# When to count the next chunk's neighbours: one visit in a chunk's last step

## The chip, the cores and the metric

The kernel runs on one core of a Trainium2 chip. The metric is the device time of one execution in microseconds (us). Three executions of the kernel before took 240.62, 241.02 and 240.00 us; the median is 240.62 us.

## The reference

Two layers of a graph network with residual and layer norm, on 4096 nodes with 64 features and a dense 0/1 adjacency matrix of 4096 x 4096, some 0.4% of it ones. Cut to what matters:

```python
# layer 0: each row's last 100 neighbours, weighted by 0.5 ** (rank from the end)
rank = jnp.cumsum(mask, axis=1)
deg = rank[:, -1:]
k = jnp.minimum(deg, 100.0)
pos = rank - (deg - k)
w = mask * jnp.where(pos > 0, 0.5 ** (k - pos), 0.0)
x = layernorm(x + (w @ (x @ weight) + bias))
# layer 1: mean over neighbours and self, linear map, relu, L2 norm
deg = sum(adj, axis=1) + 1
h = (adj @ x + x) / deg
z = relu(concat([x, h], 1) @ W + b)
x = layernorm(x + z / max(norm(z), 1e-12))
```

The weight of an edge depends on how many neighbours of its row have a higher column number. So a block of the matrix can be weighed only when the blocks of higher columns have been counted.

## The kernel before

**Tiles and steps.** The matrix is handled transposed, in 64 tiles of 512 rows (a slab g, 0 to 7) by 512 columns (k, 0 to 7). Within a slab k runs from 7 down to 0, slabs run from 0 to 7, and each tile is one step: `when[g, k]` gives the step number i, 0 to 63. A tile is read from HBM as float32 and stored as bf16 (512 KB) by a DMA that GpSimd (POOL) issues (`load_next`, L97 to L104). Eight loads are issued ahead, then one at the start of every step, so step i issues load i + 8. There are 32 tile buffers; later loads wait until the tile that holds the buffer has been used for the last time, which is in a sum of layer 1.

**Chunks.** The tiles of a slab are grouped into chunks (`chunks`, L84): one tile each in slabs 0 and 1, chunks of 1, 1, 2, 2, 2 in slab 2, chunks of two in slabs 3 and 4, and of four in slabs 5 to 7. All tiles of a chunk share one `near`: how many neighbours the row has beyond this chunk, capped. The chunk's own tiles lie close enough together that the ordering inside it is worked out from the tile itself.

**What a chunk needs before its first weighing.** `count` (L243) multiplies each of its tiles by `pick` (four matmuls a tile, 128 rows by 32 columns, into the PSUM tile `cnt`). After the chunk's last count DVE adds the result to the running sums (`cs`, L257, or L259 for the first chunk of a slab). `spread` (L262) multiplies `cs` by `further` (PSUM tile `rep`, L265), and ACT turns that into `near` (L267). `cnt`, `rep` and three small products of the epilogue (`pz`, `px`, `pu`) share two PSUM buffers in rotation.

**A step.** The order on each engine is written out by hand. On TensorE (PE) a step is: the counts of its share of the next chunk; `weigh` (L269), 16 matmuls with `tri` (L277) and 16 with `mine` and `near` (L286), 32 x 32 array tiles each, into PSUM `v`; four matmuls of layer 1 where any are ready (`some_sums`, L338, `acc_part`, L313); the `spread` if the share ended the chunk; `gather` (L299, `acc`, L304), the product of layer 0 with the step before's weights; and epilogue pieces of the slab before (`pz`, `px`, `pu`). ACT and DVE each turn half of `v` into weights `w` (L293, L294). PSUM holds `v` of one step, so a step's weighing waits until both halves of the step before's `w` are out. Where no sum of layer 1 was ready and a spread is due, half of the gather is placed ahead of the spread.

**Epilogue of layer 0.** It is spread over the eight steps that follow a slab: `pz` and `y` in the second step of the next slab, `mv` in the third, a square root `s` (ACT) and `r` (DVE) in the fourth, `x1` in the fifth, `hi` and `xl` in the sixth, `lo` and `px` in the seventh, `x1T` and `pu` in the eighth, `c1` one later. After step 63 the remaining sums of layer 1 and its epilogue follow, in an order written out by hand.

The line in the step loop that deals out the counts is L541; `ahead` is the next chunk:

```python
shares = {1: [ahead], 2: [ahead[:2], ahead[2:]], 4: [[], ahead[:2], [], ahead[2:]]}[len(chunk)]
```

In a chunk of two, the first step counts the first two tiles of the next chunk and the second step what is left of it; in a chunk of four, the second step counts two tiles and the fourth the other two.

Of the kernel before, what the change touches and what calls it, by code (L numbers as in the profile page):

```python
# [39 lines left out]
def adj_resnorm_kernel(  # L40
# [42 lines left out]

    chunks = []  # L84
    for g in range(NG):
        sizes = [1] * 8 if g < 2 else [1, 1, 2, 2, 2] if g == 2 else [2] * 4 if g < 5 else [4] * 2
        k = NK
        for n in sizes:
            chunks.append([(g, k - 1 - i) for i in range(n)])
            k -= n  # L90
# [6 lines left out]
    def load_next(n=1):  # L97
        for _ in range(n):
            s = next(loads, None)
            if s is None:  # L100
                return
            g, k = s
            a = a16p.tile([P, KB, R], BF16, tag="a16", name=f"a16_{g}_{k}")
            nc.gpsimd.dma_start(out=a, in_=adjT[g, k])  # L104
            A[g][k] = a
# [137 lines left out]
    def count(g, k, first, last):  # L243
        if first:
            cnt[g] = ps_m.tile([P, R], F32, tag="m", name=f"cnt_{g}_{k}")
        for q in range(KB):
            nc.tensor.matmul(  # L247
                cnt[g][quarters[q], :],
                lhsT=pick[:, PW - 4 * k : PW - 4 * k + Q],
                rhs=A[g][k][:, q, :],  # L250
                start=first,
                stop=last,
            )
        if last:
            new = one.tile([P, R], BF16, tag="cs", name=f"cs_{g}_{k}")
            if g in cs:
                nc.vector.tensor_tensor(new, cnt[g], cs[g], ALU.add)  # L257
            else:
                nc.vector.tensor_copy(new, cnt[g])  # L259
            cs[g] = new  # L260

    def spread(g, k):  # L262

        pr = ps_m.tile([P, R], F32, tag="m", name=f"rep_{g}_{k}")
        nc.tensor.matmul(pr, lhsT=further, rhs=cs[g], start=True, stop=True)  # L265
        near[g] = epi.tile([P, R], BF16, tag="near", name=f"near_{g}_{k}")
        nc.scalar.activation(near[g], pr, AF.Relu, bias=most, scale=-1.0)  # L267

    def weigh(g, k, nr):  # L269

        w = wp.tile([P, KB, R], I16, tag="w", name=f"w_{g}_{k}")
        v = [ps_v.tile([P, 2, R], F32, tag="v", name=f"v_{g}_{k}_{i}") for i in range(2)]
        for q in range(KB):
            for e in range(4):
                nc.tensor.matmul(  # L277
                    v[e // 2][quarters[q], e % 2, :],
                    lhsT=tri[quarters[e], :],
                    rhs=A[g][k][quarters[e], q, :],  # L280
                    start=True,
                    stop=False,
                )
        for q in range(KB):
            for e in range(4):
                nc.tensor.matmul(  # L286
                    v[e // 2][quarters[q], e % 2, :],
                    lhsT=mine[quarters[e], 4 * k + q, :],
                    rhs=nr[quarters[e], :],
                    start=False,  # L290
                    stop=True,
                )
        nc.scalar.activation(w[:, 0:2, :], v[0], AF.Relu, bias=less)  # L293
        nc.vector.tensor_scalar(w[:, 2:4, :], v[1], -STEP * MAX_NEIGH, 0.0, ALU.add, ALU.max)  # L294
        return w
# [3 lines left out]
    def gather(g, k, w, q0=0, q1=KB):  # L299
        if (k, q0) == (NK - 1, 0):  # L300
            acc0[g] = ps_a.tile([P, R], F32, tag="acc0", name=f"acc0_{g}")
        for q in range(q0, q1):
            b = k * KB + q
            nc.tensor.matmul(  # L304
                acc0[g],
                lhsT=xhl[:, b, :],
                rhs=w[:, q, :].bitcast(BF16),
                start=(k, q) == (NK - 1, 0),
                stop=(k, q) == (0, KB - 1),
            )  # L310
# [19 lines left out]
    def evict_part(g):  # L330
        acc = acc1.pop(g)
        if g in part:
            nc.vector.tensor_tensor(part[g], acc, part[g], ALU.add)
        else:
            part[g] = const.tile([P, R], F32, name=f"part_{g}")
            nc.scalar.copy(part[g], acc)

    def some_sums(i, n):  # L338

        done = None  # L340
        while n and todo and done is None and ready(i, todo[0][0], todo[0][1]):
            g, b, first, last = todo.pop(0)
            if first:
                acc1[g] = ps_a.tile([P, R], F32, tag="acc1", name=f"acc_part_{g}_{b}")
            second(acc1[g], g, b, first, last)
            n -= 1
            if last:
                done = g
        return done
# [55 lines left out]
    def first_hT(g):  # L405
        ep["hT", g] = epi.tile([P, R], F32, tag="hT", name=f"hT0_{g}")
        nc.scalar.copy(ep["hT", g], acc0[g])
# [76 lines left out]
    def run(i, engine):  # L484
        for fn, args in hooks.pop((i, engine), []):
            fn(*args)
# [36 lines left out]
    def warm(n):  # L523

        a = A[0][NK - 1][:, 0, :]
        for i in range(n):
            nc.tensor.matmul(pi, lhsT=a[:, 0:P], rhs=a, start=True, stop=True)  # L527
# [10 lines left out]
    for c, chunk in enumerate(chunks):  # L538
        ahead = chunks[c + 1] if c + 1 < len(chunks) else []

        shares = {1: [ahead], 2: [ahead[:2], ahead[2:]], 4: [[], ahead[:2], [], ahead[2:]]}[len(chunk)]  # L541
        nr = near[chunk[0][0]]
        for (g, k), share in zip(chunk, shares):
            i = when[g, k]
            run(i, ACT)
            load_next()
            run(i, POOL)

            w = weigh(g, k, nr) if i == 0 else None
            for s in share:  # L550
                count(*s, s == ahead[0], s == ahead[-1])
            w = w or weigh(g, k, nr)
            run(i, "ACT, late")
            if i == 0:
                warm(4)
            n_todo = len(todo)
            done = some_sums(i, QUOTA)
            half = 0
            if share and share[-1] == ahead[-1]:
                if held is not None and len(todo) == n_todo:  # L560

                    half = KB // 2
                    gather(*held, 0, half)
                spread(*ahead[-1])
            if i == 0:
                warm(3)
            if done is not None:
                evict_part(done)
            if held is not None:
                gather(*held, half)  # L570
            held = (g, k, w)
            if g > 0 and k == NK - 1:
                first_hT(g - 1)
            run(i, PE)
            run(i, DVE)
# [389 lines left out]
```

## Time and profile before

| what | value |
|---|---|
| median of three executions | 240.62 us |
| profiled execution, its own time | 242.02 us |
| its span, first to last instruction | 239.9 us |
| PE busy (matmuls) | 216.0 us, 90% |
| DVE busy | 177.5 us, 74% |
| ACT busy | 134.2 us, 56% |
| POOL busy | 83.4 us, 35% |
| mean granted TensorE clock | 0.967 |
| tile loads: number, median from issue to landing | 64, 15.8 us |

The busy time is an average over stages with different limits, so the stages have to be read one by one: the row of slices cuts the span into 40 equal parts and gives the busy share of each engine in tenths. The list of waits names for each waiting instruction what ended its wait. The timeline shows instructions in order of time: start, duration, engine, line, operation, output and inputs, count, and in brackets the idle time before it with what ended it.

### The profile page before, as it was taken

Reading aid. Unit: us, or ns where it says so; the run is one execution under the profiler, and the core shown is the slowest. Engines: PE = TensorE matmul, PEld = TensorE weight load, DVE = VectorE, ACT = ScalarE, POOL = GpSimd, SP = SyncE. Lnnn points to the kernel's source line nnn. Section 1 sums busy time; section 2 is a strip of 40 time slices with the busy share of each in tenths; the row PEclk is TensorE's granted clock in tenths of the full one; section 3 lists DMA queues with packets and bytes.
Section 4 is the critical chain, followed back from the end, with each engine's and each line's share of the span. In section 5 each row is a group of like instructions: output and inputs, shape, how many; then the busy total and the mean of one; then the engine's idle time right before and its main releaser. Section 6 shows DMA issues by size and latency. Waiting matters only on the chain.

```text
span 239.9 us, 7440 instructions
## 1 busy us (share of the span) xinstructions
PE 216.0 (90%) x3167; PEld 95.9 (40%) x3167; DVE 177.5 (74%) x453; ACT 134.2 (56%) x201; POOL 83.4 (35%) x160
## 2 busy tenths in 40 slices
PE   8689989999789999999999999899999999999810
PEld 2223324244323442443344334443443355676700
DVE  5458888977578689579857975686568866679983
ACT  5058876787357637665555455545555641163493
POOL 8334584331430140221223132313371000168960
PEclk9799999999899999999999999999999999999975
DMA  6999999999999999999899999999990000000021
GB/s 202 211 210 222 210 213 214 221 215 214 221 213 214 216 219 214 214 213 187 163 171 179 165 189 197 178 156 195 209 190 9 0 3 0 3 0 25 0 87 66
DMA packets 11984, 37.33 MB, mean 156 GB/s; under 512 B 1328, under 2 KB 3504, under 8 KB 11952
## 3 DMA queue, kind: packets, MB, share of 16 engines
q0 software_dynamic: 9216, 33.56, 72.6%
q1 hardware_dynamic: 2736, 3.31, 4.2%
q8 instruction: 24, 0.39, 0.6%
q14 instruction: 8, 0.07, 0.1%
HBM read 69.37 MB, written 1.05 MB: 293 GB/s over the span
## 4 chain that ended last, share of the span: by engine, by line
PE 53%; DMA 22%; DVE 11%; POOL 6%; ACT 4%; issue 2%; ACTq 0%; POOLq 0%; DVEq 0%
DMA a<-in_adjT_dram 22%; PE acc L304 14%; PE acc_part L313 13%; PE v L277 7%; PE cnt L247 4%; PE v L286 4%; ACT w L293 3%; PE va L313 2%; DVE w L294 2%; POOL r L377 2%; PE pi L527 2%; PE pz L413 2%; PE rep L265 2%; POOL rn L377 2%; PE va L658 1%
## 5 line engine op out<-in xcount | busy, mean ns | idle before, releaser
L293 ACT ACTIVATE w<-v,less 128x1024 int16<-128x1024 f32 x64 | 71.3, 1115 | 56.3 <-PE v L286 42.5
L294 DVE TENSOR_SCALAR w<-v 128x1024 int16<-128x1024 f32 x64 | 78.3, 1223 | 24.9 <-PE v L286 23.8
L104 POOL DMA_DIRECT2D a<-in_adjT_dram x64 | 36.0, 564 | 103.6 <-PE acc_part L313 44.4
L304 PE MATMUL acc<-w,xhl 128*128 128x512 bf16 x256 | 70.1, 384 | 0.0
L313 PE MATMUL acc_part<-a,x1hl 128*128 128x512 bf16 x156 | 40.5, 382 | 0.0
L304 PEld LDWEIGHTS <-xhl 128*128 128x128 f16 x256 | 23.1, 98 | 35.4 <-issue 12.0
L313 PEld LDWEIGHTS <-x1hl 128*128 128x128 f16 x224 | 18.6, 98 | 30.6 <-issue 13.8
L277 PE MATMUL v<-a,tri 32*32 32x512 bf16 x1024 | 29.5, 388 | 0.7 <-ACT w L293 0.6
L267 ACT ACTIVATE near<-rep,most 128x512 bf16<-128x512 f32 x35 | 23.9, 683 | 9.1 <-PE rep L265 9.1
L247 PE MATMUL cnt<-a,pick 128*32 128x512 bf16 x256 | 22.1, 387 | 7.0 <-DMA a<-in_adjT_dram 6.5
L286 PE MATMUL v<-near,mine 32*32 32x512 bf16 x1024 | 28.3, 380 | 0.0
L257 DVE TENSOR_TENSOR cs<-cnt,cs 128x512 bf16<-128x512 f32 x27 | 18.5, 685 | 8.8 <-PE cnt L247 8.8
L277 PEld LDWEIGHTS <-tri 32*32 32x32 bf16 x1024 | 9.8, 88 | 22.2 <-issue 21.6
L265 PE MATMUL rep<-cs,further 128*128 128x512 bf16 x35 | 13.8, 393 | 2.2 <-DVE cs L257 2.1
L377 POOL TENSOR_TENSOR rn<-ss,power 128x4 f32<-128x4 f32 (+1 forms) x5 | 6.3, 1277 | 26.2 <-DVE ss L680 26.2
L247 PEld LDWEIGHTS <-pick 128*32 128x32 bf16 x256 | 5.1, 93 | 21.7 <-issue 15.2
L232 POOL TENSOR_TENSOR a<-a,ident_b 128x128 bf16<-128x128 bf16 x32 | 12.7, 428 | 0.1
L286 PEld LDWEIGHTS <-mine 32*32 32x32 bf16 x1024 | 9.9, 88 | 1.8 <-issue 1.8
L658 PE MATMUL va<-wts,hT 128*128 128x64 f32 x64 | 8.0, 276 | 2.2 <-ACT hT L631 1.1
L259 DVE CAST cs<-cnt 128x512 bf16<-128x512 f32 x8 | 5.5, 690 | 5.4 <-PE cnt L247 5.4
L209 POOL TENSOR_TENSOR xr<-c,xhl 128x256 f32<-128x256 f32 x8 | 5.3, 664 | 11.7 <-ACT xhl L207 11.6
L747 ACT ACTIVATE u<-u,off,r 128x64 f32<-128x64 f32 x24 | 8.6, 431 | 0.8 <-POOL off L736 0.8
(136 smaller groups left out, 236.9 us busy)
## 6 DMA issues: line engine op xcount, KB each, us to landing
a<-in_adjT_dram POOLq DMA_DIRECT2D x64, 512.0 KB, 15.8
c<-in_x_quads_dram SPq DMA_DIRECT2D x2, 512.0 KB, 4.5
x<-in_x_dram SPq DMA_DIRECT2D x8, 128.0 KB, 6.4
out_dram<-u SPq DMA_DIRECT2D x8, 128.0 KB, 1.7
wts<-in_weights_dram SPq DMA_DIRECT2D x1, 160.0 KB, 7.2
```

The source lines that it names most:

```text
L104: nc.gpsimd.dma_start(out=a, in_=adjT[g, k])
L247: nc.tensor.matmul(cnt[g][quarters[q], :], lhsT=pick[:, PW - 4 * k : PW - 4 * k + Q], rhs=A[g][k][:, q, :], start=first, stop=last,)
L257: nc.vector.tensor_tensor(new, cnt[g], cs[g], ALU.add)
L265: nc.tensor.matmul(pr, lhsT=further, rhs=cs[g], start=True, stop=True)
L267: nc.scalar.activation(near[g], pr, AF.Relu, bias=most, scale=-1.0)
L277: nc.tensor.matmul(v[e // 2][quarters[q], e % 2, :], lhsT=tri[quarters[e], :], rhs=A[g][k][quarters[e], q, :], start=True, stop=False,)
L286: nc.tensor.matmul(v[e // 2][quarters[q], e % 2, :], lhsT=mine[quarters[e], 4 * k + q, :], rhs=nr[quarters[e], :], start=False, stop=True,)
L293: nc.scalar.activation(w[:, 0:2, :], v[0], AF.Relu, bias=less)
L294: nc.vector.tensor_scalar(w[:, 2:4, :], v[1], -STEP * MAX_NEIGH, 0.0, ALU.add, ALU.max)
L304: nc.tensor.matmul(acc0[g], lhsT=xhl[:, b, :], rhs=w[:, q, :].bitcast(BF16), start=(k, q) == (NK - 1, 0), stop=(k, q) == (0, KB - 1),)
L313: nc.tensor.matmul(acc, lhsT=x1hl[:, b, :], rhs=A[g][b // KB][:, b % KB, :], start=first, stop=last)
L377: nc.gpsimd.tensor_tensor(r, v, power[:, 0:n], ALU.pow)
```

## The change

Two edits. The counts of the next chunk are all made in the last step of a chunk, in one visit, ahead of that step's weighing, and the spread follows in the same step. For a chunk of one nothing changes; for a chunk of two the counts move from its first step to its second; for a chunk of four the first half joins the second half in the fourth step. And slab 4's last two chunks of two become one chunk of four.

```diff
-        sizes = [1] * 8 if g < 2 else [1, 1, 2, 2, 2] if g == 2 else [2] * 4 if g < 5 else [4] * 2
+        sizes = {0: [1] * 8, 1: [1] * 8, 2: [1, 1, 2, 2, 2], 3: [2] * 4, 4: [2, 2, 4]}.get(g, [4, 4])
...
-        shares = {1: [ahead], 2: [ahead[:2], ahead[2:]], 4: [[], ahead[:2], [], ahead[2:]]}[len(chunk)]
+        shares = [[]] * (len(chunk) - 1) + [ahead]
```

## The prediction

> **What bounds the kernel now.** I read the slices first. The profile row for DMA tells where transfers run without a gap, PEclk where TensorE went cold.
>
> ```profile
> PE   8689989999789999999999999899999999999810
> PEclk9799999999899999999999999999999999999975
> DMA  6999999999999999999899999999990000000021
> GB/s 202 211 210 222 210 213 214 221 215 214 221 213 214 216 219 214 214 213 187 163 171 179 165 189 197 178 156 195 209 190 9 0 3 0 3 0 25 0 87 66
> ```
>
> A slice is 6.0 us. Until 108 us (18 slices) the queue moves 202 to 222 GB/s without a break; then the rate falls to 156 to 209 while PE stays full. So there are two stages: up to about 74 us a tile's landing sets the pace (the chain of waits has DMA pieces from 24.4 to 63.1 us), afterwards PE does, up to 210 us. The list of waits then says what each engine waited for (total us, times, longest):
>
> ```profile
> PE cnt L247 <- DMA a<-in_adjT_dram: 6.5, 9, 2.2
> PE rep L265 <- DVE cs L257: 2.1, 3, 1.1
> POOL a L104 <- PE acc_part L313: 44.4, 20, 4.6
> ```
>
> PE's only large wait is that of a count for a tile not yet landed. POOL's 44.4 us says that late loads are issued when a sum of layer 1 frees a buffer, so they follow PE. The timeline shows the wait that this change moves:
>
> ```profile
> 60.92 0.40 PE L247 MATMUL cnt<-a,pick 128*32 128x512 bf16 x4
> 63.06 0.40 PE L247 MATMUL cnt<-a,pick 128*32 128x512 bf16 x4 [1.74 <-DMA a<-in_adjT_dram]
> 63.39 0.46 PE L277 MATMUL v<-a,tri 32*32 32x512 bf16 x16
> ...
> 71.17 0.38 PE L265 MATMUL rep<-cs,further 128*128 128x512 bf16 x1 [1.10 <-DVE cs L257]
> ...
> 152.55 0.40 PE L247 MATMUL cnt<-a,pick 128*32 128x512 bf16 x4 [0.62 <-DMA a<-in_adjT_dram]
> ```
>
> At 60.92 PE is in step 18 (steps are numbered from 0, eight to a slab; pz of slab 1 at 59.91 marks step 17). It counts tiles 20 and 21, waits 1.74 us for tile 21, and its own weighing, whose tile is long there, stands behind the count. At 152.55 (step 49) the first half of a split visit waits for tile 53.
>
> **The Trainium skill.** "TensorEngine Tiling (Array Packing)", Key Properties: changing the tiling mode drains TensorE. The trace agrees: a visit with one tile moves the next operation by 0.33 us (20.38 to 20.71), one with two tiles by 0.54 (101.73 to 102.27). So a tile costs 0.21 and a visit 0.12 beside it. "TensorE: Matmul & The Clock Gate", Part 1: an idle stretch throttles the clock. After the 1.74 us the granted clock in 60 to 66 us is 0.81. The same page, Architectural detail: ScalarE and VectorE take instructions strictly in order. In the trace near always follows its step's w (104.15 after 103.07 plus 1.11).
>
> **Part 1, what goes away.** Visits before: 18 chunks of one tile, 11 of two, six of four in two visits: 41. After: 18 + 9 + 7 = 34. Seven visits at 0.12 are 0.84 us of PE. One chunk fewer saves a spread (0.22 us of PE: acc starts 0.22 after rep), a cs on DVE (0.69) and a near on ACT (0.68). All 256 count matmuls stay. SP's and POOL's instructions and their order stay; only when buffers come free moves.
>
> **Part 2, the landing wait, steps 18 to 24.** Chunks of two were counted in their predecessor's first step and now in its last, one step later. Load n+8 waits until load n has landed, so POOL's issue times give landings: tile 21 at 63.06 (the count), 22 at 66.0, 23 at 68.5, 24 at 71.3, 25 at 73.7. These stay. I walk PE with the durations of the timeline: tri and mine 0.58 from start to next operation, four gathers or sums 0.86, ACT's w ends 1.91 after v starts, DVE's 2.09.
> - Step 18: v at 60.95 instead of 63.39, gather to 62.4.
> - Step 19 counts tiles 20 and 21: waits from 62.6 to 63.06; v 63.4. DVE first ends mv (63.9), then cs (64.6), so rep 64.7, near 65.6 to 66.3 (behind w and the square root).
> - Step 20: v waits for w of step 19 (65.9), mine for near (66.35).
> - Step 21 counts 22, 23: waits for 68.5, v 68.8, rep 69.9, near to 71.45.
> - Step 22: mine waits for near (71.5), gather and px to 73.1. Step 23 counts 24, 25: waits for 73.7, v 74.1, sums, rep, gather, pu to 77.0.
> - Step 24: v at 77.1 against 79.95 before. But before, tiles 26 and 27 had been counted then (0.54), and the spread is level. Net gain 2.3.
>
> **Part 3, steps 25 to 36.** Steps 27 to 29 have no sums to run, and there ACT and DVE set the pace: w alone takes 1.91 to 2.09 of a step whose PE work is 1.53. Now cs and near of the next chunk fall into steps 27 and 29 with the square root, r and hi: rep at 27 and at 29 waits some 0.4 each for cs, mine at 28 and 30 some 0.2 for near, and v at 28 and 30 for DVE's w. Step 31's v comes at 97.65 against 99.08; one spread of 0.22 is behind, so the gain is down to 1.2. Step 35 now counts four tiles, in 0.97 us from 109.4; the last, tile 39, lands at 109.0 (load 39 issued at 101.0, 8.0 to landing), just in time. Step 37's v: 115.1 against 116.4, gain **1.3** (the spread saved is in it).
>
> **Part 4, steps 37 to 63.** PE-bound, sums in every step, and the visits at 39, 43, 47 and so on already ended with spread in the last step, so near's chain is as before. Six visits go (39, 41, 45, 49, 53, 57): 6 x 0.12 = 0.7. The visit at 49 took 1.35 us from 151.53 to 152.88 instead of 0.54; that 0.8 goes, if no later count waits in its place. Step 51 needs tile 55: issued at 151.04, landed 6.8 later, 157.8; counted at 158.69. The step 49 work that goes shortens the lead from 7.65 to about 7.0 at the last tile's turn, against 6.8: it just holds. Tile 51 at step 47 (issued 139.41, 6.5 to landing) has about 6.2 and waits 0.3. Sum: 0.7 + 0.8 - 0.3 = **1.2**, rounded down to 1.1.
>
> **What is not shown.** The waits of near at a chunk's first step are bounded by 0 (hidden) and by 0.68 each (whole near exposed); I take 0.2 to 0.45 from the walk in the four boundaries without sums and 0 elsewhere, because with sums near ends 2.57 us after v (104.84) and mine of the next step starts 2.86 after. The landing waits of slabs 5 to 7 lie between 0 and 1.0 per visit (the 0.62 seen, and more if the queue backs up); I take 0.3 in all. They can also be under today's: 0.2 at 145.5 may vanish. POOL's adds may lengthen a DVE operation by up to 0.8 (q_l took 0.97 at 68.88 against 0.16 at 91.21); the same either way.
>
> **Sum.** 1.3 + 1.1 = 2.4 us. The profiled execution took 242.02 us (span 239.9 and 2.1 around it), 1.4 above the median of 240.62; its 2.4 us are taken off the median: **238.2**. What follows 182 us (own sums, last epilogue) moves earlier as a whole: it has no load left to wait for.
>
> **Rivals.**
> 1. The chain costs are hidden too (ACT and DVE catch up as mv and x1 no longer share steps with cs). The waits of part 2 and 3 that I charged come to about 2.0 (0.8 for cs, 1.2 for near). Without them: 236.2. For it: y and mv stood beside cs in one step (86 to 90 us). Against: 1.10 at 71.17 shows that this chain is already exposed. Chance 0.12.
> 2. The landing wait only moves. Steps 19, 21, 23 wait at the same landings, and what PE did earlier is lost by ACT and DVE before 100 us. Then only part 4 is left, 0.5 to 1.2: 239.4 to 240.1. For it: transfers run unbroken to 108 us, so no landing moves. Against: from 74 us a PE step takes 2.4 to 2.9 us and a tile 2.45, so PE keeps its lead. Chance 0.19.
> 3. Slower: spread in the last step puts count, cs, rep and near in a row before the next weighing, behind ACT's w, at each of the nine boundaries that a chunk of two now leaves this way. It decides from 0.5 us a boundary, as 9 x 0.5 eats the 4.4 that would be won without it; at the whole near, 0.7, it is 6.3 - 4.4 = 1.9 slower: 242.5. For it: rep waits on cs at 71.17 and 92.69, and ACT is 90% busy in slices 4 and 5. Against: slabs 0 and 1 have had this order in every step. Chance 0.17.
> That the change does not do what it says is ruled out by the instruction order: 34 visits, each with its spread in the same step.
>
> **Numbers.** My forecast has 0.52, with its own range 237.2 to 239.3. About 0.5%, 1.2 us, is what a measurement of this kernel can tell from no change. Faster by more: my case, rival 1: 0.64. Within: rival 2: 0.19. Slower: rival 3, 0.17. Range 236.2 (rival 1) to 241.8 (part of rival 3).
>
> **What would show it.** Right: count wait at step 18 gone, v of step 18 near 61, waits at 63 and 68.5 instead; PEclk no longer 8 in slice 10; v of step 24 near 77 (pu just ahead), of step 37 near 115; no count visit in the 49th step and its 0.62 wait gone; last load issued some 2 us earlier than 175.1. Wrong: rep waiting for cs, or mine for near, above 4 us in all; counts at steps 47, 51 or 55 waiting for their fourth tile above 1 us each; or a step 37 no earlier than 116.

## The result

The changed kernel takes 239.89 us (median of 22 runs, 238.12 to 242.84) against 240.66 us before (22 runs, 239.63 to 242.12). The ratio is 0.9964, 95% interval 0.9941 to 0.9987: 0.4% faster, where 1% was forecast. Medians and ranges here are those of all runs, while a ratio leaves out the runs more than 1.5% above the fastest of their kernel (four of the 22 here; the means differ by 0.4 us with them and by 0.9 without). The profiled execution took 239.26 us, span 237.5 us, so by the spans of these two executions (239.9 before) the forecast of 2.4 us was met; the median says otherwise, and the scatter has doubled: 4.7 us between the fastest and the slowest run against 2.5. Both are taken up below.

The slices of the changed kernel:

```profile
PE   8589979989989999999999999999799999998810
PEclk9799999999999999999999999999999999999995
DMA  6999999999999999999899999999990000000021
GB/s 201 208 214 221 215 213 214 222 214 214 222 213 214 213 220 215 215 212 214 195 181 197 158 207 189 197 160 177 178 186 5 0 3 0 3 0 25 0 88 66
```

PEclk no longer shows an 8 in slice 10, the 60 to 66 us in which TensorE was cold before. And PE has a 7 where before had a 9, late in the run: slice 28, 166.3 to 172.2 us (one slice is 5.94 us). The list of waits has the line of the counts almost unchanged:

```profile
PE cnt L247 <- DMA a<-in_adjT_dram: 6.7, 8, 2.6
```

The total is 6.7 against 6.5 us, so as a sum nothing went away. Its place changed, which the timeline shows:

```profile
60.91 0.43 PE L277 MATMUL v<-a,tri 32*32 32x512 bf16 x16
...
62.46 0.84 PE L247 MATMUL cnt<-a,pick 128*32 128x512 bf16 x8
...
68.30 0.40 PE L247 MATMUL cnt<-a,pick 128*32 128x512 bf16 x4 [0.61 <-DMA a<-in_adjT_dram]
...
76.34 0.43 PE L277 MATMUL v<-a,tri 32*32 32x512 bf16 x16
...
113.96 0.53 PE L277 MATMUL v<-a,tri 32*32 32x512 bf16 x16 [0.35 <-ACT w L293]
...
165.24 0.83 PE L247 MATMUL cnt<-a,pick 128*32 128x512 bf16 x12
167.72 0.40 PE L247 MATMUL cnt<-a,pick 128*32 128x512 bf16 x4 [1.65 <-DMA a<-in_adjT_dram]
```

Step 18 weighs at 60.91, with no count ahead of it any more. Step 24 weighs at 76.34 (79.95 before), step 37 at 113.96 (116.34). Then, in step 55, the visit for four tiles has done three (x12) and waits 1.65 us for the fourth, tile 59. The chain that ended last now has a load there:

```profile
159.70 7.98 DMA a<-in_adjT_dram
```

Issued at 159.70, it landed 7.98 us later. Before, the same load took 5.6.

### The profile page after: what moved, and what is told of

The parts are those of the page before. It is cut to its first block, busy times and chain, and to the rows that moved or that the text cites. A ratio compares the mean times of both kernels' runs of the same rounds, so it can differ in the third digit from the quotient of the medians.

```text
span 237.5 us, 7391 instructions
## 1 busy us (share of the span) xinstructions
PE 209.7 (88%) x3123; PEld 97.0 (41%) x3166; DVE 176.7 (74%) x452; ACT 133.5 (56%) x200; POOL 82.7 (35%) x160
## 4 chain that ended last, share of the span: by engine, by line
PE 42%; DMA 36%; issue 8%; DVE 6%; POOL 5%; ACT 2%; ACTq 0%; POOLq 0%
DMA a<-in_adjT_dram 36%; PE acc L304 10%; PE acc_part L313 9%; PE v L277 5%; PE cnt L247 3%; PE v L286 3%; PE va L313 2%; POOL r L377 2%; POOL rn L377 2%; PE rep L265 1%; PE pi L527 1%; PE va L658 1%; PE vb L313 1%; PE ma L313 1%; PE pz L413 1%
## 5 line engine op out<-in xcount | busy, mean ns | idle before, releaser
L104 POOL DMA_DIRECT2D a<-in_adjT_dram x64 | 35.4, 554 | 102.1 <-PE acc_part L313 43.2
L304 PE MATMUL acc<-w,xhl 128*128 128x512 bf16 x242 | 65.9, 380 | 1.8 <-issue 1.0
L313 PE MATMUL acc_part<-a,x1hl 128*128 128x512 bf16 x130 | 36.8, 381 | 2.4 <-issue 1.8
L247 PE MATMUL cnt<-a,pick 128*32 128x512 bf16 x256 | 21.4, 389 | 7.4 <-DMA a<-in_adjT_dram 6.7
L267 ACT ACTIVATE near<-rep,most 128x512 bf16<-128x512 f32 x34 | 23.2, 681 | 8.3 <-PE rep L265 8.3
L286 PE MATMUL v<-near,mine 32*32 32x512 bf16 x1024 | 27.4, 376 | 0.1
L257 DVE TENSOR_TENSOR cs<-cnt,cs 128x512 bf16<-128x512 f32 x26 | 17.8, 685 | 5.2 <-PE cnt L247 5.0
L247 PEld LDWEIGHTS <-pick 128*32 128x32 bf16 x256 | 6.1, 94 | 22.5 <-issue 15.2
L265 PE MATMUL rep<-cs,further 128*128 128x512 bf16 x34 | 13.1, 386 | 1.1 <-DVE cs L257 1.0
L658 PEld LDWEIGHTS va<-wts,hT 128*128 128x128 f32 x64 | 7.6, 191 | 3.4 <-DVE hT L626 1.9
```

The source lines that it names most:

```text
L247: nc.tensor.matmul(cnt[g][quarters[q], :], lhsT=pick[:, PW - 4 * k : PW - 4 * k + Q], rhs=A[g][k][:, q, :], start=first, stop=last,)
L286: nc.tensor.matmul(v[e // 2][quarters[q], e % 2, :], lhsT=mine[quarters[e], 4 * k + q, :], rhs=nr[quarters[e], :], start=False, stop=True,)
L304: nc.tensor.matmul(acc0[g], lhsT=xhl[:, b, :], rhs=w[:, q, :].bitcast(BF16), start=(k, q) == (NK - 1, 0), stop=(k, q) == (0, KB - 1),)
L313: nc.tensor.matmul(acc, lhsT=x1hl[:, b, :], rhs=A[g][b // KB][:, b % KB, :], start=first, stop=last)
L658: nc.tensor.matmul(pz[:, t, :], lhsT=h[:, ts(b % TB, P)], rhs=wn_sb, start=True, stop=True)
```

## The experiments

**What they have to tell apart.** Theory A: the early gain is real, and late landings take most of it back. Theory B: it was luck of one execution, or PE pays for the visits elsewhere. Theory C: the profiled spans are right and the medians noisy. All runs are compared with the kernel before on the same chip; the medians of before lay between 240.59 and 240.80 us.

**Once more, and the change in parts.** The first run is the changed kernel again. Two runs each move the visits of one chunk size, one makes only the edit of the sizes:

```diff
 # twos last
-shares = {1: [ahead], 2: [ahead[:2], ahead[2:]], 4: [[], ahead[:2], [], ahead[2:]]}[len(chunk)]
+shares = {1: [ahead], 2: [[], ahead], 4: [[], ahead[:2], [], ahead[2:]]}[len(chunk)]
 # fours last
+shares = {1: [ahead], 2: [ahead[:2], ahead[2:]], 4: [[], [], [], ahead]}[len(chunk)]
 # slab 4 only: the new line of sizes, the old line of shares
```

> The changed kernel once more. Theory A (landing): the early stage gains about 2.5 us by step 37 in every run; in slabs 5 to 7 the one visit for four tiles (steps 47, 51, 55) waits for its fourth tile, a different step and 1 to 3 us in each run, so 239 to 240.5 us and a wider spread than before. Theory B (early): the gain by step 37 was luck of one execution; step 37's v comes at 115 to 116.5 here. Theory C (noise): the true gain is the 2.4 us of the profiled spans; 238.2 us.

> Only the chunks of two count in their last step; chunks of four keep two visits, slab 4 keeps [2, 2, 2, 2]. Theory A: the early gain of some 2.5 us stays and the late counts wait no more than before: 238.0 to 238.6 us, ratio 0.990. Theory B: no gain from chunks of two: 240.3 to 241 us. Theory C: somewhat behind the changed kernel, as six visits and a chunk fewer are missing, 239 us.

> Only the chunks of four count in one visit; chunks of two as before, slab 4 as before. Theory A: six visits fewer save 0.7 us and landing waits take 0.5 to 2 back: 240.3 to 242 us, ratio 1.000 to 1.006. Theory B: this is where the gain comes from, 239.9 us. Theory C: 0.7 us of visits and the 0.6 wait at step 49 go, 239.4 us.

> Only the edit of the sizes: slab 4 is [2, 2, 4], shares as before. All theories: one spread (0.22 us of PE), one visit, one cs and one near less, 0.3 us, ratio 0.998 to 1.000. If tiles 38 and 39 counted at step 35 (landing 109.0) make PE wait, up to 0.5 us slower instead.

| run | median us (runs) | ratio, 95% interval |
|---|---|---|
| changed kernel again | 239.85 (22) | 0.9967, 0.9944 to 0.9989 |
| twos last | 237.95 (6) | 0.9904, 0.9877 to 0.9931 |
| fours last | 241.57 (22) | 1.0013, 0.9991 to 1.0034 |
| slab 4 only | 239.29 (22) | 0.9962, 0.9944 to 0.9979 |

The changed kernel came out the same, so theory C falls. In its profiled execution, the longest of its 22, step 37's v comes at 114.41, where theory B had 115 to 116.5. Late counts wait 0.49 us at step 51 and 1.93 at step 55, and after the second the granted clock is 0.53 from 171 to 174 us: step 55 then takes 4.54 us, in the first profile 2.86. So in this execution the late landing cost more than its wait, which adds to the scatter. A part of the change is better than the whole: with only the chunks of two moved, the gain is the full 1.0% and all six runs but one lie within 0.3 us. The other part, one visit for four tiles, gains nothing. The timeline of its profiled execution, one of the longer ones, has the same wait at the same step 55:

```profile
170.76 0.40 PE L247 MATMUL cnt<-a,pick 128*32 128x512 bf16 x4 [1.95 <-DMA a<-in_adjT_dram]
```

Twos last has no landing wait after 80 us. That is as theory A has it. Slab 4 alone saves 0.9 by its ratio and not the 0.3 foreseen; against the base of the last experiment below, 239.69, it is 0.4 (only three of its 22 runs had the cold clock described there, a mean of at most 0.971, and 23 of the 59 of the kernel before on that chip).

**The late landings made cheap.** Of the tiles of slabs 5 to 7 only half is loaded, and each half is read twice, so these slabs compute with other data, but every engine does as many instructions on as much of it, and only the late transfers move half the bytes. The edit was made to both kernels:

```diff
-            nc.gpsimd.dma_start(out=a, in_=adjT[g, k])
+            n = KB if g < 5 else KB // 2
+            nc.gpsimd.dma_start(out=a[:, 0:n, :], in_=adjT[g, k][:, 0:n, :])
 # in count, weigh, second, own_half and add_self: block q % 2 instead of q for g >= 5
```

> The kernel before, but of the tiles of slabs 5 to 7 only the first half is loaded and used twice (so those slabs compute with other data; every engine's instructions stay, the late loads move half the bytes). This is the base for the next run. All theories: only its own late landing waits go (0.6 at step 49): 239.6 to 240.6 us.

> The changed kernel with the same halved late loads. Theory A (late landings take the gain back): without them the whole gain shows: step 56's v some 4 us earlier than in the base, 235.5 to 236.5 us. Theory B (the visits for four tiles cost PE time themselves, in waits of near or in the order on ACT and DVE): the gain stays under 1 us against the base, 239 us or more.

The base took 240.04 us (22 runs, ratio to before 0.9994, 0.9975 to 1.0012), the changed kernel 238.22 us (6 runs, 237.70 to 238.65; ratio 0.9902, 0.9873 to 0.9932). From 120 to 190 us the waits of PE in the changed kernel with half loads are a single line, with no DMA in it, and the scatter is gone too (1.0 us between its six runs):

```profile
PE v L281 <- ACT w L297: 0.2, 1, 0.2
```

So landings cost the changed kernel 239.85 - 238.22 = 1.6 us at the median, and the kernel before 240.59 - 240.04 = 0.5 (0.1 by the ratio), which its interval can't tell from nothing. The gain itself is not the 4 us that I expected here but 1.8. From the two profiles: step 37's v 114.36 against 115.40 in the base, step 60's 181.24 against 183.14; 1.0 us from the early stage, 0.9 from there on, where the visits are saved.

**Why do the same tiles land later?** Three runs keep the early part and slab 4's chunk of four, and deal out the counts of a chunk of four differently:

```diff
-shares = [[]] * (len(chunk) - 1) + [ahead]
 # fours split
+shares = {1: [ahead], 2: [[], ahead], 4: [[], ahead[:2], [], ahead[2:]]}[len(chunk)]
 # fours each
+... 4: [ahead[j : j + 1] for j in range(4)] ...
 # fours adjacent
+... 4: [[], [], ahead[:2], ahead[2:]] ...
```

> The changed kernel, but chunks of four count in two halves again (second and fourth step); chunks of two in their last step and slab 4 as [2, 2, 4]. Theory A: the early gain (2.3 us, as with only the chunks of two moved), the chunk saved (0.3 to 0.7), no late landing waits: 237.0 to 237.8 us, faster than the changed kernel and than the run with only the chunks of two moved. Theory B: the same.

> As the run before, but a chunk of four counts one tile of the next in each of its four steps: the same lead for every tile, the evenest spacing of PE's steps, ten visits more (1.2 us of PE). Theory A, if it is the bunching of short steps after a visit for four that delays landings: no late landing waits, and 1.0 to 1.4 us above the run before. If instead the fourth tile waits simply because its lead is too short, this run waits as the changed kernel does and takes 239 us or more.

> As the run with fours split (chunks of two in their last step, slab 4 as [2, 2, 4]), but a chunk of four makes its two visits in its third and fourth step instead of its second and fourth. As many visits, and the last tile has the same lead. If bunching matters (two short steps in a row release two loads faster than they are served, so the next ones land later), the last tile of some chunk waits 0.3 to 1 us and the time lies between the split run and the changed kernel, 238.4 to 239.5 us. If only a visit for four tiles is late, no waits and 238.0 to 238.4 us.

| run | median us (runs) | ratio, 95% interval |
|---|---|---|
| fours split | 238.24 (6) | 0.9901, 0.9872 to 0.9930 |
| fours each | 240.87 (22) | 1.0017, 0.9999 to 1.0035 |
| fours adjacent | 240.94 (22) | 1.0011, 0.9988 to 1.0034 |

Fours split and fours adjacent have the same number of visits, and in both the last tile of a chunk is issued and counted in the same steps. Yet adjacent is 2.7 us slower at the median, twice what was expected at most, and its timeline has two late waits where that of split has none:

```profile
156.40 0.40 PE L247 MATMUL cnt<-a,pick 128*32 128x512 bf16 x4 [0.83 <-DMA a<-in_adjT_dram]
...
168.73 0.40 PE L247 MATMUL cnt<-a,pick 128*32 128x512 bf16 x4 [0.96 <-DMA a<-in_adjT_dram]
```

These are steps 51 and 55, in each of which the second half waits for the chunk's last tile; they are 1.8 of the 2.6 us between the two profiles' spans. What differs is when the loads are issued and how long each takes. From the traces, start of issue and time to landing in us:

```
load                 57           58           59           60           61
before           158.1  5.6   161.1  5.6   163.7  5.6   166.7  5.3   169.1  5.9
changed          153.7  7.4   157.1  7.7   159.7  8.0   162.1  8.1   164.5  8.1
fours split      154.2  6.1   157.2  5.7   159.9  5.7   162.8  7.2   165.2  6.6
fours adjacent   154.7  7.8   158.7  7.1   161.3  7.4   163.7  8.2   166.7  7.2
```

A load is issued when a step's sums free a buffer, so the gaps between issues are PE's steps. In fours split every second step carries a visit: the gaps in the table are 2.4 to 3.0 us, with no two short ones in a row, and the loads land in 5.7 to 7.2. In the changed kernel a gap of 3.4 is followed by 2.6, 2.4, 2.4, and each load lands some 2 us later than before. The lead of tile 59, from its issue to its turn in the count, is 6.4 us in the changed kernel, 6.3 in split and 6.5 in adjacent; only where it lands in 5.7 is it in time. So it is shown that dealing out the same visits to other steps turns punctual landings into late ones. That the spacing of the issues does it is the reading that fits best: in the five profiles with one visit for four tiles, or with two visits in the third and fourth step, load 59 took 7.2 to 8.3 us, in six of the other seven with whole loads 5.3 to 5.7. But the spacing does not decide it alone. Loads 57 and 58 of the changed kernel are late already ahead of the short gaps. Its loads 49 to 51 came after the same gaps as 57 to 59 (3.3, 3.4, 2.6) and landed in 5.2 to 6.1. And the seventh profile, that of the last experiment below, has the gaps of fours split from load 48 to load 59, within 0.1 us, yet its load 59 took 7.8. What else has to come together stays open.

Fours each has the evenest steps, and in its profile one late wait, of 0.3 us. Its step 60 comes 2.06 us after that of split: 1.19 from step 40 on, with ten more visits and the late wait, and 0.87 up to there, with two more visits and a wait of 0.15 for tile 39. That is more than the 1.0 to 1.4 expected, which had ten visits and nothing else; at the median it is 2.6.

**A suspect that explains little.** The x blocks of slabs 6 and 7 are transferred between the late tiles. In two runs the x blocks of slabs 5 to 7 are fetched at steps 27 to 29:

```diff
-        at(NK * g + 3, POOL, load_x, g)
+        at(NK * g + 3 if g < 5 else 22 + g, POOL, load_x, g)
```

> The changed kernel, but the x blocks of slabs 5 to 7 are loaded at steps 27 to 29 instead of at steps 43, 51 and 59. If it is these transfers that hold up the tiles of slabs 5 to 7 (tile 52 landed 4.1 to 5.1 us after tile 51 with the change), the late landing waits go and the time is 238.0 to 238.6 us. If it is the pace of the releases, they stay: 239.3 to 240 us.

> The run with fours split, with the same early x blocks. It has no late waits to lose: 237.7 to 238.4 us in either theory; anything above 238.6 would be the early x blocks delaying tiles in the first stage, and would have to be taken off the run before.

They took 240.79 us (ratio 1.0000, 0.9976 to 1.0024) and 241.48 us (1.0017, 0.9992 to 1.0042). The early blocks hold up a tile of the first stage: both wait 1.45 us at step 35 for tile 39 (110.63 us). Taking that off leaves the first at about 239.3, half a microsecond under the changed kernel, which the intervals can't tell from nothing, and its profile (one of its longer executions) still has late waits, 0.85 at step 55 and 1.33 at step 59. So the x blocks are at most a part of the cause. In the second run the loads 48 to 63 take 5.6 us to land on average, in fours split 6.2; but in twos last, with the x blocks where they were, it is 5.6 as well. The second was expected at 238.4 at most and came out 3.2 us above split; 1.5 of it is that wait, the rest is open (its profiled execution is one of its shortest and has no late wait).

**The base and its cold clock.** Profiles of code that is identical up to step 34 disagree by 1 us at step 22: v at 74.70 in before, 73.72 in slab 4 only. In the first the granted clock fell to 0.81 after the 1.74 us wait of step 18, in the second it stayed at 1.00. So seven matmuls were put into that wait:

```diff
+            if i == 18:
+                pi2 = ps_a.tile([P, R], F32, tag="acc1", name="pi2")
+                for j in range(7):
+                    nc.tensor.matmul(pi2, lhsT=A[g][k][:, 0, 0:P], rhs=A[g][k][:, 0, :], start=True, stop=True)
             for s in share:
                 count(*s, s == ahead[0], s == ahead[-1])
```

> The kernel before, with seven matmuls of 128 x 128 x 512 (1.5 us, into a PSUM tile that nobody reads) ahead of the count of step 18, so that TensorE is busy in most of the 1.74 us in which it waited for tile 21. If the granted clock falls because of that wait (0.81 in 60 to 66 us of the profiled execution of before, 1.00 in other profiles of the same code), it stays at 1.00 here, the square root of slab 1 comes 1 us earlier and step 22's v is at 73.7 and not 74.7: the median falls to 239.7 to 240.2 us and the upper half of the runs thins out. If the clock's fall has another cause, the time stays at 240.6 or rises a little.

239.69 us (22 runs), ratio 0.9963, 0.9945 to 0.9981, and 19 of the 22 runs lie between 239.43 and 239.79. By this metric seven matmuls that compute nothing are worth as much as the whole change. In the kernel before, 12 of 27 runs on that chip had a mean granted clock of at most 0.971, and their spans were 1.0 us longer than those of the others (238.96 and 237.94 on average); with the seven matmuls no run of 22 had. That the wait leads to the cold clock, and the cold clock to the longer span, is so shown. It isn't all of the difference: averaged over all runs the device time falls by 0.8 us and the span by 0.3; the rest lies outside the span and is open. The profiled execution, one of the three longer ones, has late landings although it counts chunks of four in two visits, as before:

```profile
169.52 0.40 PE L247 MATMUL cnt<-a,pick 128*32 128x512 bf16 x4 [0.91 <-DMA a<-in_adjT_dram]
```

This is load 59 with its 7.8 us.

Why the cold clock costs 1 us shows in three lines of the timeline of before:

```profile
68.56 0.29 ACT L357 ACTIVATE s_l<-mv_l,eps_ln 128x4 f32<-128x4 f32 x1
68.88 0.97 DVE L363 TENSOR_TENSOR q_l<-s_l 128x4 f32<-128x4 f32 x1
69.08 0.74 POOL L237 TENSOR_TENSOR x<-x,wts 128x256 f32<-128x256 f32 x1
```

and in the same ones with TensorE kept busy:

```profile
67.42 0.29 ACT L357 ACTIVATE s_l<-mv_l,eps_ln 128x4 f32<-128x4 f32 x1
67.74 0.16 DVE L363 TENSOR_TENSOR q_l<-s_l 128x4 f32<-128x4 f32 x1
...
69.19 0.74 POOL L237 TENSOR_TENSOR x<-x,wts 128x256 f32<-128x256 f32 x1
```

The slower matmuls delay the square root by 1.14 us. DVE's next operation, 0.16 us by itself, then falls into POOL's addition and ends with it (69.85 and 69.82). cs stands behind it on DVE, and rep waits 1.10 for cs. The Trainium skill, "SBUF — State Buffer", section "Who interferes with whom", describes such a case: a VectorE instruction with two SBUF inputs contends with a GpSimd instruction that reads SBUF, and the one that is issued first blocks the other for its whole duration. The trace agrees in that the two end together (in fours last, which was cold too, at 69.90 and 69.87). The order it doesn't show: the record of DVE's operation begins 0.20 us before that of the addition.

## Why the prediction was wrong in size

**Direction and range** held: 239.89 lies in 236.2 to 241.8, and it is faster. But 2.4 us were forecast and 0.8 measured, below the 0.5% that I took as a bound.

**Part 1** held. A visit was put at 0.12: from step 40 to 48 the changed kernel with half loads takes 23.07 us, fours split 23.29, with two visits more, so 0.11 each.

**Part 2** held, a little on the safe side. Step 18's v was put at 60.95 and came at 60.91; step 23's v was put at 74.1, after a wait for tile 25, and came at 73.48 with no wait that the list shows; step 24's v was put at 77.1 and came at 76.34. near was late at steps 20 and 22, as walked.

**Part 3** lost too much: step 37's v was put at 115.1 and came at 113.96. The gain of 2.4 in the profiles was 1.3 in the sum. But 0.9 of the 2.4 belongs to the base: its profiled execution was one with the cold clock, and in the warm one with half loads step 37's v comes at 115.40 and not at 116.34. Against that the gain is 1.0 (114.36, half loads) to 1.4 (113.96), so the 1.3 agrees with a warm base, which is not the one it was worked out from. I had read the 0.81 in the slices and not asked whether every execution has it. The page of the Trainium skill that was cited, "TensorE: Matmul & The Clock Gate", Part 1, lets the clock fall after an idle window of about 3.4 us and says that this window runs freely. At step 18 waits of half that length, 1.60 to 1.74 us, were followed by a lower clock in two profiles and not in two others; where that differs from the page, the measurement holds.

**Part 4 failed**, in its last term, the 0.3 us for late landings. It rests on "Tile 51 at step 47 ... has about 6.2 and waits 0.3", and on tile 55 at step 51: "against 6.8: it just holds". In the first profile both are in time (tile 55 landed in 6.4; in the second profile it took 7.5 and the count waited 0.49). What failed is that I took the times to landing of before, 5.6 to 6.8, for fixed. Tile 59, with 5.6 before, I had not walked at all: its lead was 6.4 us from issue (159.70) to its turn (166.07), enough for 5.6 but not for the 8.0 that it took. The change bunches PE's steps, and with them the issues; as far as known, that is why loads land later. Landing waits cost 1.6 us at the median and not 0.3. With late landings made cheap the changed kernel takes 238.22 us, where the sum without this term gives 237.9.

**The rivals.** Rival 2 named the time, 239.4 to 240.1, by the wrong mechanism: the early lead was not lost before 100 us. It was still there at step 54 (162.60 against 167.17); at step 56 it is 2.3 us (170.91 against 173.22), and of the 2.3 lost 1.65 are the one wait, while most of the rest is counting that before had already done at step 53. Rival 3's chain of cs, rep and near came to 0.3 us of rep waiting for cs after 80 us. (The 90% for ACT in slices 4 and 5 that was held for it is a misreading: no slice of ACT in the profile of before is above 8 tenths.) The paragraph on what is not shown had the right wait, with 0 to 1.0 per visit as its bounds; 1.65 was outside them.

**The better version** is the part: chunks of two in their last step, chunks of four in two visits. With slab 4 as before it took 237.95 us, with the chunk of four in slab 4 238.24 (237.0 to 237.8 had been expected); between these two, with six runs each, the runs don't decide.

## What to carry to other kernels

Where loads are issued by the buffers that compute frees, the order of compute sets the spacing of the loads: an edit that makes some steps long and others short can make transfers land later, just where the next long step needs them. Here 5.6 us became 8.0. So don't price a landing at its old duration when an edit moves the issues; leave it a margin, and walk every count that waits for a recent load. And before a gain is read from one profile, ask whether the base of that profile is a typical execution; here the granted clock by slice told.

## What the runs showed of the hardware

- A wait of 1.60 to 1.74 us with the same code was followed by a granted clock of 0.81 and 0.76 (60 to 66 us) in two profiles and of 1.00 in two others. With seven matmuls in the wait no run of 22 had a mean clock of 0.971 or less, where 12 of 27 had before, and the kernel before became 0.9 (ratio) to 1.1 us (median) faster.
- With two or three loads outstanding the rate of the transfers varies: in the changed kernel 111, 143, 188, 111 and 115 GB/s in the five microseconds from 158 to 163 us, but 190 to 231 in the six from 138 to 144; in the first stage, up to 108 us, it was 214 on average. What makes the slow stretches stays open, and with it the inside of the late landings.
